# Guarding 48 small sums of squares on ScalarE instead of VectorE, in a four-block transformer kernel

## The chip, the cores and the metric

The kernel runs on one core of a Trainium2 chip. The core has five engines that each take their instructions in order: TensorE (PE, matrix products), VectorE (DVE), ScalarE (ACT), GpSimd (POOL) and SyncE (SP, which here only issues transfers). They work side by side and wait for each other through semaphores. Matrix products are written to PSUM, everything else lies in SBUF. The metric is the device time of one execution in microseconds (us); the figure before is the median of three runs.

## The reference

The input x is [4, 512, 128] in fp32. Four blocks follow each other, each as `x = x + layernorm(block(layernorm(x)))`: a linear attention, a stack of six layers of local attention and feed-forward, a dense causal attention with a softsign-like score, and a gated feed-forward. The change lies in the stack. Its attention layer, cut to what matters:

```python
def l2norm(t):
    return t / jnp.maximum(jnp.linalg.norm(t, axis=-1, keepdims=True), 1e-12)

for i in range(6):                          # 16 heads of 64, window 32
    q, k, v = split_heads(x @ Wqkv[i])
    q = rotary(l2norm(q) * q_scale[i], scale)
    k = rotary(l2norm(k) * k_scale[i], 1 / scale)
    sim = (q @ k_two_windows.T) * 8.0       # masked
    x = softmax(sim) @ v_two_windows @ Wo[i] + x
    x = ffn(layernorm(x)) + x               # gelu gate
```

For every token and head the kernel needs 1 / max(norm, 1e-12) of 64 numbers of q and of k. It takes the sum of squares, keeps it from being under 1e-24 (the guard), and forms the inverse root as exp(-0.5 ln(sum)).

## The kernel before, in words

The stack is written out as a list of steps k: six layers, four batches, two halves of eight heads (`steps`, L294), 48 in all. Each k is spread over four inner steps, so that s runs over 192 score steps, with a lead-in of ten and a tail. The loop at L681 runs over s under a manual schedule: the order of the code is the order on each engine. In each s it advances several k at once, by the offsets in `inside(s, n)`:

- `score` and `exponentials` (offset 0): for one pair of heads, a mask product (L443) and 32 small products q k (L453) into the tile sc, which has one buffer in PSUM; then VectorE's maxima (L460) and `top` (L463), and eight ACTIVATEs pr on ScalarE in two groups of four (L70), each followed by a read of the accumulator. The next s's mask product can start only when the second group of four is done.
- `project`, `rotate`, `squares`, `squared`, `rotated` (offset 10): two projections pp a step (L307), for each a multiplication by the rotary tables on VectorE (L318, tile t), the squares on ScalarE (L329, tile sq), the sums of squares over 64 columns on VectorE (L343, into ss) and the addition of the rotated halves on GpSimd (L339, tile r).
- `guarded`, `norms`, `refined`, `normed` (offset 6): the block that is changed. For each k, at its first s (`first`, when s mod 4 is 2), VectorE guards ss, 128 x 64 numbers for q and k and four token tiles, and multiplies by -0.5 (L351); ScalarE takes Ln with scale -2 and Exp with scale -0.5 (both through the helper at L70), into rn; GpSimd refines rn by one Newton step (L365 to L368, with ss again), and multiplies the keys by it (L374).
- `turn_k` (offset 4): four transposes tp on TensorE (L387), and a copy kT on ScalarE. `value` (offset 2): a product pv (L420) and a copy vn (L424).
- Offsets -1 to -4: `by_key` and `in_place` lay out the softmax weights, `weighted` forms av (L513), the copy attn (L736) takes it out of PSUM, `output` adds the product with Wo (L521).
- `parts`: the feed-forward of one layer and batch, spread over eight s by the list LATE (L526): transposes pt and px, the normalisation xt, the affine xg (L564), products pg with gelu (L578), pa (L589) and py (L599), residual additions on VectorE (L532, L606).

The period of the loop is therefore eight s: two k, one feed-forward. At s mod 8 = 7 the two copies attn and vn go to VectorE (L687); else they are on ScalarE. The PSUM tiles pp, tp, pv, pt, px, pg, pa share one pool of three banks (`mm`, L288) that go round in the order of use.

What stands in the order of the code around the change: within one s with a norm block, VectorE does the first sum of squares (L719), then the guard, then the second rotary multiplication (L733). ScalarE does the second four exponentials (L726), Ln and Exp (L728), the copies attn and vn, and the second squares (L740).

Of the kernel before, what the change touches and what calls it, by code (L numbers as in the profile page):

```python
# [8 lines left out]
F32 = mybir.dt.float32  # L9
I32 = mybir.dt.int32  # L10
BF16 = mybir.dt.bfloat16
AF = mybir.ActivationFunctionType
ALU = mybir.AluOpType
# [3 lines left out]
P = 128  # L17
# [14 lines left out]
def sandwich(ctx: ExitStack, tc: tile.TileContext, a: dict, out: bass.AP):  # L32

    nc = tc.nc
# [29 lines left out]
    def table_act(out, in_, func, **kw):  # L64
        if SETS[func] != phase["set"]:
            load_set = nc.scalar.preload_act_table_set(SETS[func])
            for name in () if phase["kept"] else phase["used"]:
                tc.add_manual_dep(load_set.ins, name, NOSYNC, reason="table phase")
            phase.update(set=SETS[func], load=load_set.ins.name, used=[])
        done = nc.scalar.activation(out, in_, func, **kw)  # L70
        if not phase["kept"]:
            tc.add_manual_dep(done.ins, phase["load"], NOSYNC, reason="table phase")
        phase["used"].append(done.ins.name)
# [24 lines left out]
    cp = stack.enter_context(tc.tile_pool(name="f0c", bufs=1))  # L98
# [31 lines left out]
    with tc.tile_pool(name="a0w", bufs=1) as awp, tc.tile_pool(name="a0", bufs=4) as work, \  # L130
# [22 lines left out]
        nc.gpsimd.tensor_copy(identb, ident)  # L153
        mhalf = cp.tile([P, 4], F32, name="mhalf")
        nc.gpsimd.memset(mhalf, -0.5)
        upper = cp.tile([P, 1], F32, name="upper")
        nc.gpsimd.memset(upper, 1.5)
        minus = cp.tile([P, 1], F32, name="minus")
# [128 lines left out]
    with tc.tile_pool(name="f0", bufs=2) as work, \  # L287
# [38 lines left out]
        def squares(k, j):  # L326
            o = proj[k]
            sq = o["sq"][j] = work.tile([P, S], F32, tag="ln_sd", name="sq")
            nc.scalar.activation(sq, o["pp"], AF.Square)  # L329
# [18 lines left out]
        def guarded(k):  # L348

            ss = proj[k]["ss"]  # L350
            nc.vector.tensor_scalar(ss, ss, 1e-24, -0.5, ALU.max, ALU.mult)  # L351

        def norms(k):

            o = proj[k]
            rn = o["rn"] = work.tile([P, 2, 4, 8], F32, bufs=3, name="rn")
            table_act(rn, o["ss"], AF.Ln, scale=-2.0)
            table_act(rn, rn, AF.Exp, scale=-0.5)
# [44 lines left out]
        def place_q(k, n):  # L403


            o = proj[k]
            if n == 0:
                o["qT"] = work.tile([P, 4, 4, 4, 32], F32, name="qT")
            for f in range(4):
                nc.sync.dma_start(  # L410
                    out=o["qT"][32 * f : 32 * f + 32, n], in_=o["qb"][32 * n : 32 * n + 32, f]
                )
# [21 lines left out]
        def score(k, p):  # L434


            o = proj[k]
            sc = scp.tile([P, 2, S], F32, tag="sc", name="sc")
            scores = o["sc"] = sc[:, :, 0 : 4 * KW].rearrange("p e (j k) -> p e j k", k=KW)
            for w in range(4):  # L440
                for e in range(2):
                    rows = slice(64 * e, 64 * e + 64)
                    nc.tensor.matmul(  # L443
                        sc[32 * w : 32 * w + 32, e, 0 : 4 * KW],
                        lhsT=identb[rows, 64 * e : 64 * e + 32], rhs=mask[rows, int(w == 0)],
                        start=True, stop=False, skip_group_check=True,
                    )
            for j in range(4):
                for w in range(4):
                    q0 = j * P + w * WIN  # L450
                    for e in range(2):
                        rows = slice(64 * e, 64 * e + 64)
                        nc.tensor.matmul(  # L453
                            scores[32 * w : 32 * w + 32, e, j, :],
                            lhsT=o["qT"][rows, w, p, j, :],
                            rhs=o["kT"][rows, p, q0 : q0 + KW],
                            start=False, stop=True, skip_group_check=True,
                        )
            raw = sc[:, 0, 4 * KW : 4 * KW + 8].rearrange("p (e j) -> p e j", e=2)
            nc.vector.tensor_reduce(raw, scores, AX.X, ALU.max, negate=True)  # L460
            top = o["top"] = work.tile([P, 2, 4], F32, name="top")
            o["rq"] = o["rn"][:, 0, :, 2 * p : 2 * p + 2]
            nc.vector.tensor_tensor(top, raw, o["rq"].rearrange("p j e -> p e j"), ALU.mult)  # L463
            o["pr"] = work.tile([P, 2, 4, KW], F32, name="pr")
            o["den"] = work.tile([P, 2, 4], F32, name="den")
# [171 lines left out]
        def inside(s, ahead):  # L637

            k, q = divmod(s + ahead, 4)
            return (k, q) if 0 <= k < len(steps) else None  # L640

        def parts(s, some):
            for part in some:
                g, left = divmod(s - LATE[part - 1], 8)
                if left or not 1 <= g <= DEPTH * NB:
                    continue
                if part < 10 or part > 13:
                    ff_part(*divmod(g - 1, NB), part)
                elif g > NB * (DEPTH - 1):
                    residual((g - 1) % NB, part - 9)  # L650
# [29 lines left out]
        with tc.manual_schedule():  # L680
            for s in range(-10, LAST + max(LATE) + 1):  # L681
                here, rot, before, flip = (inside(s, n) for n in (0, 10, 9, 9))
                fold, place, turn, val = (inside(s, n) for n in (6, 5, 4, 2))
                first = fold and fold[1] == 0

                copy = nc.scalar.copy
                if s % 8 == LATE[5] % 8 and LATE[5] < s:  # L687
                    copy = nc.vector.tensor_copy
                if place:
                    place_q(*place)  # L690
                if here:
                    score(*here)
                parts(s, (2, 5, 7, 8))
                if rot:
                    project(rot[0], 2 * rot[1])
                if here:
                    exponentials(here[0], 0)
                if rot:
                    rotate(rot[0], 2 * rot[1])
                    squares(rot[0], 2 * rot[1])  # L700
                if before:
                    squared(before[0], 2 * before[1] + 1)
                if turn:
                    turn_k(*turn)
                parts(s, (9,))
                back = inside(s, -4)
                if back:
                    i, b, hf = steps[back[0]]
                    c = 4 * hf + back[1]
                    if c == 0:  # L710
                        ff["py"] = pyp.tile([P, S], F32, name="py")
                    output(i, c, attn, ff["py"])
                if s - 1 in fresh:
                    by_keys[s - 1] = by_key(fresh.pop(s - 1))
                parts(s, (1, 3, 15))
                if s - 2 in by_keys:
                    in_place(*by_keys[s - 2])
                if rot:
                    squared(rot[0], 2 * rot[1])  # L719
                    rotated(rot[0], 2 * rot[1])  # L720
                if first:
                    guarded(fold[0])
                if rot:
                    project(rot[0], 2 * rot[1] + 1)
                if here:
                    exponentials(here[0], 1)  # L726
                if first:
                    norms(fold[0])  # L728
                back = inside(s, -3)
                if back:  # L730
                    av = weighted(*back, by_keys.pop(s - 3)[0])
                if rot:
                    rotate(rot[0], 2 * rot[1] + 1)  # L733
                if back:
                    attn = work.tile([P, S], F32, tag="attn", bufs=1, name="attn")
                    copy(attn.rearrange("p (j h c) -> p j h c", j=4, h=2), av)  # L736
                if val:
                    value(*val, copy)
                if rot:
                    squares(rot[0], 2 * rot[1] + 1)  # L740
                parts(s, (4,))
                if flip:
                    flip_q(*flip)
                if rot:
                    rotated(rot[0], 2 * rot[1] + 1)
                if here:
                    fresh[s] = normalise(here[0])
                if first:
                    refined(fold[0])
                if fold:  # L750
                    normed(*fold)
                parts(s, (14, 6, 10, 11, 12, 13))
                if here:
                    weights(*divmod(s, 32))
# [6 lines left out]
    with tc.tile_pool(name="f1w", bufs=1) as gp, tc.tile_pool(name="a1w", bufs=1) as wp, \  # L761
# [18 lines left out]
        scale = 1.0 / DH1**0.5 * 16.0  # L780
# [419 lines left out]
```

## Time and profile before

| | |
|---|---|
| median of three runs | 1991.85 us (1987.7, 1991.85, 2001.1) |
| the profiled execution | 1998.52 us, of which the span from the first to the last instruction is 1996.8 us |
| PE, DVE, ACT, POOL busy | 1812.8, 1624.7, 1603.7, 1549.5 us |
| granted TensorE clock, mean over the span | 0.957 of full |
| from 500 to 800 us: PE, DVE, ACT, POOL busy | 292.85, 268.15, 261.44, 265.13 of 300 us |
| guard L351 on DVE | 48 times, 22.2 us; 179 ns least, 182 median, 1291 most |
| Ln and Exp of the norm on ACT | 48 times each, 14.2 and 12.3 us |

In a line of a timeline the first number is the start in us from the start of the span, the second the duration in us; then engine, source line, operation, output tile <- input tiles, partitions x elements, count. A bracket at the end is the idle time of that engine just before, and what ended it. Consecutive instructions of an engine overlap a little in the profile, so a duration is somewhat longer than the distance to the next start. In a line of a group the busy time in us and the mean of one in ns follow the count, and after the second bar the idle time before them. A TensorE product of this size is two instructions, and its end is modelled.

### The profile page before, as it was taken

The numbers are of one execution on the slowest core, as the hardware profiler recorded it, in microseconds if no ns is written. First come the engines' busy times: TensorE is split into PE (matmuls) and PEld (weight loads), VectorE is DVE, ScalarE is ACT, GpSimd is POOL, SyncE is SP. The second block draws the span as 40 slices with busy tenths as digits, with TensorE's granted clock in tenths as the row PEclk, the third lists the DMA queues.
The fourth block names the chain that finished last, engine by engine and source line by source line (L and its number), as shares of the span: only waits on it lengthen the run. The fifth ranks groups of instructions, "written<-read, shape, count | busy, mean of one in ns | idle before, by whom it ended". The sixth has DMA issues, their size and how long they took to land.

```text
span 1996.8 us, 75926 instructions
## 1 busy us (share of the span) xinstructions
PE 1812.8 (91%) x30648; PEld 951.5 (48%) x30648; DVE 1624.7 (81%) x2561; ACT 1603.7 (80%) x4645; POOL 1549.5 (78%) x2026
## 2 busy tenths in 40 slices
PE   6779899999999999999999999999998877878878
PEld 3235455555555555555555555555555423323323
DVE  3698788888988898998888998889984369888833
ACT  3458788888888888888888888888888639988953
POOL 1279888888988889888898888988886338878850
PEclk9889999999999999999999999999999968889889
DMA  3023443344433444334434335333333110000000
GB/s 99 0 66 95 114 118 80 94 109 117 105 95 84 108 116 110 97 79 116 126 92 100 97 100 133 95 84 97 92 91 96 34 46 1 1 1 1 1 0 21
DMA packets 98892, 155.27 MB, mean 78 GB/s; under 512 B 29552, under 2 KB 56944, under 8 KB 93936
## 3 DMA queue, kind: packets, MB, share of 16 engines
q1 hardware_dynamic: 98544, 150.43, 29.6%
q8 instruction: 243, 3.98, 0.9%
q14 instruction: 105, 0.86, 0.2%
HBM read 23.44 MB, written 1.05 MB: 12 GB/s over the span
## 4 chain that ended last, share of the span: by engine, by line
PE 54%; ACT 19%; DVE 16%; issue 4%; SPq 4%; DMA 3%; POOL 1%; DVEq 0%; POOLq 0%; ACTq 0%
PE pp L307 10%; ACT pr L70 8%; PE av L513 6%; PE pv L420 5%; PE sc L453 5%; PE py L521 5%; PE pa L589 4%; PE pg L578 3%; PE py L599 3%; DVE la L899 3%; DVE t L318 3%; DVE lb L897 2%; ACT sq L329 2%; PE tp L387 2%; PE sc L443 2%
## 5 line engine op out<-in xcount | busy, mean ns | idle before, releaser
L70 ACT ACTIVATE pr<-sc,top,rn 128x64 f32<-128x64 f32 x1536 | 607.8, 420 | 84.5 <-DVE top L463 32.0
L339 POOL TENSOR_TENSOR r<-t 128x512 f32<-128x512 f32 x384 | 486.5, 1276 | 150.4 <-DVE t L318 132.5
L318 DVE TENSOR_TENSOR t<-pp,tab 128x1024 f32<-128x1024 f32 x384 | 467.9, 1219 | 42.8 <-PE pp L307 33.2
L307 PE MATMUL pp<-wqkv,z 128*128 128x512 f32 x768 | 412.2, 620 | 13.3 <-ACT sq L329 8.8
L70 ACT ACTIVATION_READ_ACCUMULATOR pr<-sc,top,rn 128x1 f32 x1536 | 336.3, 219 | 0.0
L329 ACT ACTIVATE sq<-pp 128x512 f32<-128x512 f32 x384 | 234.0, 609 | 89.6 <-DVE t L318 87.1
L343 DVE TENSOR_REDUCE ss<-sq 128x8 f32<-128x512 f32 x384 | 257.1, 669 | 6.6 <-ACT sq L329 4.3
L513 PEld LDWEIGHTS av<-pT,ve 64*64 64x64 f32 x6144 | 165.4, 134 | 154.6 <-POOL pT L502 46.0
L907 POOL TENSOR_TENSOR lb<-lb,la 128x2048 f32<-128x2048 f32 x40 | 182.7, 4567 | 53.8 <-issue 34.2
L420 PE MATMUL pv<-wqkv,z 128*128 128x512 f32 x384 | 217.0, 647 | 3.4 <-ACT sq L329 3.4
L479 POOL TENSOR_TENSOR pr<-pr,den 128x512 f32<-128x512 f32 x192 | 201.0, 1047 | 24.3 <-DVE den L478 22.9
L460 DVE TENSOR_REDUCE sc<-sc 128x8 f32<-128x512 f32 x192 | 131.5, 685 | 93.6 <-PE sc L453 93.0
L513 PE MATMUL av<-pT,ve 64*64 64x32 f32 x6144 | 197.6, 222 | 8.8 <-DMA qT<-qb 5.3
L307 PEld LDWEIGHTS pp<-wqkv,z 128*128 128x128 f32 x768 | 135.0, 193 | 146.5 <-issue 108.1
L374 POOL TENSOR_TENSOR r<-r,rn 128x512 f32<-128x512 f32 x192 | 200.8, 1046 | 3.8
L521 PE MATMUL py<-attn,wo 128*128 128x512 f32 x384 | 197.0, 594 | 1.5 <-ACT attn L736 1.5
L513 PE MATMUL av<-pT,vn 64*64 64x32 f32 x6144 | 193.7, 219 | 0.0
L453 PE MATMUL sc<-kT,qT 64*32 64x64 f32 x12288 | 171.1, 223 | 8.7 <-issue 8.7
L503 POOL COPY pT<-blocks 32x256 f32<-32x256 f32 x384 | 152.4, 397 | 22.3
L513 PEld LDWEIGHTS av<-pT,vn 64*64 64x64 f32 x6144 | 166.3, 135 | 0.1
L453 PEld LDWEIGHTS sc<-kT,qT 64*32 64x32 f32 x12288 | 154.5, 105 | 10.0 <-issue 9.5
L502 POOL COPY pT<-blocks 32x256 f32<-32x256 f32 x384 | 150.3, 391 | 11.1 <-issue 2.9
(195 smaller groups left out, 3271.2 us busy)
## 6 DMA issues: line engine op xcount, KB each, us to landing
qT<-qb SPq DMA_DIRECT2D x768, 64.0 KB
ve<-vn SPq DMA_DIRECT2D x48, 768.0 KB
pT<-blocks SPq DMA_DIRECT2D x768, 32.0 KB
wqkv<-in_f_wqkv SPq DMA_DIRECT2D x36, 256.0 KB
ve<-vn SPq DMA_DIRECT2D x48, 192.0 KB
tab<-in_rot SPq DMA_DIRECT2D x12, 256.0 KB
wo<-in_f_wo SPq DMA_DIRECT2D x6, 512.0 KB
ve<-vn SPq DMA_DIRECT2D x48, 64.0 KB
```

Of the source, the lines that this page charges most:

```text
L70: done = nc.scalar.activation(out, in_, func, **kw)
L307: nc.tensor.matmul(pp, lhsT=z[b][:, WIN + t * P : WIN + (t + 1) * P], rhs=ws[i]["qkv", hf][:, n * S : (n + 1) * S], start=True, stop=True,)
L318: nc.vector.tensor_tensor(t12, o["pp"].rearrange("p (h d) -> p h d", d=DH0).unsqueeze(1) .to_broadcast([P, 2, 8, DH0]), ws[i][f"tab{n}"][: ...
L329: nc.scalar.activation(sq, o["pp"], AF.Square)
L339: nc.gpsimd.tensor_tensor(r, t1, t2[:, :, ::-1, :], ALU.add)
L343: nc.vector.tensor_reduce(o["ss"][:, n, t, :], o["sq"].pop(j).rearrange("p (h d) -> p h d", d=DH0), AX.X, ALU.add,)
L374: nc.gpsimd.tensor_tensor(v, v, o["rn"][:, 1, t].unsqueeze(2).to_broadcast([P, 8, DH0]), ALU.mult)
L420: nc.tensor.matmul(pv, lhsT=z[b][:, WIN + t * P : WIN + (t + 1) * P], rhs=ws[i]["qkv", hf][:, 2 * S :], start=True, stop=True,)
L453: nc.tensor.matmul(scores[32 * w : 32 * w + 32, e, j, :], lhsT=o["qT"][rows, w, p, j, :], rhs=o["kT"][rows, p, q0 : q0 + KW], start=False, ...
L479: nc.gpsimd.tensor_tensor(o["pr"], o["pr"], o["den"].unsqueeze(3).to_broadcast([P, 2, 4, KW]), ALU.mult)
L513: nc.tensor.matmul(av[64 * e : 64 * e + 64, h, 64 * j + 32 * c : 64 * j + 32 * c + 32], lhsT=vs[c][rows, j, (2 * p + e) * DH0 : (2 * p + e ...
L521: nc.tensor.matmul(py, lhsT=ws[i]["wo"][:, c, :], rhs=t, start=(c == 0), stop=(c == 7))
```

## The change

The guard no longer runs on VectorE. In its place ScalarE does two operations in front of Ln. The first is Relu(ss - 1e-24), the second is Identity(-0.5 y - 0.5e-24), which gives -0.5 max(ss, 1e-24) together. Both take their constant from a column of a new tile `under`, which GpSimd fills at the start. The call of `guarded` moves from between the first sum of squares and the second projection to just in front of `norms`, behind the second group of exponentials. Ln then waits for ScalarE's own Identity in place of VectorE's guard, and Relu waits for VectorE's last sum of squares of that k, which is early in the same s.

```diff
         mhalf = cp.tile([P, 4], F32, name="mhalf")
         nc.gpsimd.memset(mhalf, -0.5)
+        under = cp.tile([P, 2], F32, name="under")
+        nc.gpsimd.memset(under[:, 0:1], -1e-24)
+        nc.gpsimd.memset(under[:, 1:2], -0.5e-24)
...
         def guarded(k):
             ss = proj[k]["ss"]
-            nc.vector.tensor_scalar(ss, ss, 1e-24, -0.5, ALU.max, ALU.mult)
+            nc.scalar.activation(ss, ss, AF.Relu, bias=under[:, 0:1])
+            nc.scalar.activation(ss, ss, AF.Identity, bias=under[:, 1:2], scale=-0.5)
...
                     rotated(rot[0], 2 * rot[1])
-                if first:
-                    guarded(fold[0])
                 if rot:
                     project(rot[0], 2 * rot[1] + 1)
                 if here:
                     exponentials(here[0], 1)
                 if first:
+                    guarded(fold[0])
                     norms(fold[0])
```

## The prediction

> **What bounds the kernel now.** I read the page first (shares, slices, chain), then the chain of waits in order of time, then the timelines of TensorE, ScalarE, VectorE and GpSimd around single instances of the changed step, and last the groups of the instructions involved.
>
> ```profile
> PE 1812.8 (91%) x30648; PEld 951.5 (48%) x30648; DVE 1624.7 (81%) x2561; ACT 1603.7 (80%) x4645; POOL 1549.5 (78%) x2026
> PE   6779899999999999999999999999998877878878
> PEclk9889999999999999999999999999999968889889
> PE 54%; ACT 19%; DVE 16%; issue 4%; SPq 4%; DMA 3%; POOL 1%; DVEq 0%; POOLq 0%; ACTq 0%
> ```
>
> The stack is the stretch from about 105 to 1510 us. TensorE (PE) is full there and has its full clock, so the time is lost or won where TensorE stalls. The chain names ScalarE (ACT) second. From 500 to 800 us TensorE is busy 292.9 of 300 us, VectorE (DVE) 268.2, ScalarE 261.4, GpSimd (POOL) 265.1: four engines at nearly 90%, so small shifts decide.
>
> The steps repeat in periods of eight (one layer and batch), near 60 us. The norm block runs twice in each: at s mod 8 = 6 ("place six") and s mod 8 = 2 ("place two"). ScalarE and TensorE at place six, s=78:
>
> ```profile
> 722.45 0.25 ACT L70 ACTIVATION_READ_ACCUMULATOR pr<-sc,top,rn 128x1 f32 x1
> 722.61 0.26 ACT L70 ACTIVATE rn<-ss 128x64 f32<-128x64 f32 x1
> 722.89 0.26 ACT L70 ACTIVATE rn<-rn 128x64 f32<-128x64 f32 x1
> 723.06 0.57 ACT L736 COPY attn<-av 128x512 f32<-128x512 f32 x1
> 723.52 0.59 ACT L424 COPY vn<-pv 128x512 f32<-128x512 f32 x1
> 724.00 0.61 ACT L329 ACTIVATE sq<-pp 128x512 f32<-128x512 f32 x1
> 724.49 0.79 ACT L564 ACTIVATE xg<-px,par 128x512 f32<-128x512 f32 x1
> ...
> 723.63 0.66 PE L562 MATMUL px<-ident,xt 128*128 128x128 f32 x4
> 724.17 1.13 PE L307 MATMUL pp<-wqkv,z 128*128 128x512 f32 x2
> ```
>
> The reader is to see that ScalarE has no gap here, and that the vn copy ends at 724.11 and the next pp product starts at 724.17. In the built program that product waits for this very copy: the three mm banks go round, and it takes the bank that the copy empties. So TensorE is already level with ScalarE at place six. I looked at the 21 such places from s=14 to s=174: in 16 the product starts 0.05 to 0.13 us after the copy, in 2 (s=62, 102) 0.35 and 0.44 us after, in 3 (s=46, 126, 166) 1.0 to 1.2 us after.
>
> **Removed: the guard on VectorE.**
>
> ```profile
> L351 DVE TENSOR_SCALAR ss<-ss 128x64 f32<-128x64 f32 x48 | 22.2, 462 | 0.0
> L70 ACT ACTIVATE rn<-ss 128x64 f32<-128x64 f32 x48 | 14.2, 295 | 1.7 <-DVE ss L351 1.7
> 721.29 1.28 DVE L351 TENSOR_SCALAR ss<-ss 128x64 f32<-128x64 f32 x1
> 722.49 1.21 DVE L318 TENSOR_TENSOR t<-pp,tab 128x1024 f32<-128x1024 f32 x1
> 721.26 1.26 POOL L339 TENSOR_TENSOR r<-t 128x512 f32<-128x512 f32 x1
> 781.62 0.18 DVE L351 TENSOR_SCALAR ss<-ss 128x64 f32<-128x64 f32 x1
> ```
>
> The guard takes 0.18 us in 31 of 48 cases, but over 1 us in 13: at 721.29 it starts 0.03 us after a GpSimd addition and ends with it. The Trainium skill ("SBUF — State Buffer", Who interferes with whom) says that a tensor_scalar can take the port pair that VectorE shares with GpSimd, as an exclusive lock, and that the later one blocks for the other's whole instruction. The rows agree (1.28 against 1.26 us). By that rule the change frees 22.2 - 48 x 0.18 = 13.6 us of stalls, and with 0.09 us of issue for each guard (752.24 to the next start at 752.33) about 18 us of VectorE. If VectorE set the end that would be 18 us won. The trace has the test in it. Of the 21 places six, 13 have a long guard and 8 a short one. From the mask product (L443) of step 7 to that of step 8 it is 9.36 us at best and 9.37 at the median with a long guard (9.38 at s=78, 722.75 to 732.13), and 9.36 at best and 9.37 at the median with a short one. One microsecond of VectorE is worth nothing there, since its next critical product, top, waits for the scores from TensorE, and ScalarE is still busy with xg when top is ready. At place two the guard is always short, and VectorE waits for TensorE before its maxima (0.18 us at 754.43). ScalarE waited for the guard 1.7 us in all, in the two runs ahead of the first scores. I take the removal at 0; bounds 18 us won and 0. What it does move is GpSimd's second addition of r at place six (1.26 us idle at 723.78, waiting for L318), up to 1.2 us earlier; the next one waits for a new pp anyway.
>
> **Added: Relu and Identity on ScalarE.** 48 of each, 128x64, each with a bias column and waiting for the one before it. The trace has no Relu; the nearest rows are the two ACTIVATEs of the same shape and the same kind of chain: Ln to Exp, start to start, is 0.28 to 0.34 us but for one of 0.40, median 0.33. In front of the chain two more links cost 2 x 0.33 = 0.66 us. The low bound is 2 x 0.28 = 0.56. For the high bound I take the Identity that has two columns (L555, four in 1.64 us at 716.99): 2 x 0.41 = 0.82. A rule of the Trainium skill speaks against the change: "ScalarE: Activation LUTs", Rules for kernel authors, sends relu, max, add and mul to VectorE. The same page (What ACT_TABLE_LOAD costs) gives an ACTIVATE with a bias column as 280 + 0.833 N ns, 333 at N = 64, with 93 of it overlapped back to back: an estimate of 0.48 us for the two. The trace's dependent pair doesn't overlap like that, so I keep 0.66. Busy time grows by 48 x 2 x 0.3 = 29 us, to about 82% of the span; what matters is where it lies.
>
> The pair stands behind the exponentials whose end releases the next scores, so that release doesn't move. Queued behind it are Ln, Exp, the attn and vn copies, sq, and xg at place six. Who waits for these:
>
> Place six: the pp product of step 7 waits for vn with nothing to spare. 16 x 0.66 = 10.6 us, less 0.1 for the two looser ones; s=62 pays 0.66 - 0.30 = 0.36 and s=102 pays 0.27; three pay nothing. Together 11.1 us. It isn't paid twice: ScalarE runs the same 0.66 us late through the gelu group of step 7 up to the exponentials of step 8. I find no later slack that takes it back, since TensorE goes from px at 723.63 to step 9 with hardly a gap, and what stalls it later (step 5) hangs on pp products that move along.
>
> Place two: ScalarE has a gap of 0.17 us before the exponentials of step 3, which takes 0.17; 0.49 goes on to the scores of step 4. The tp transposes of step 3 wait for vn and have about 0.45 to spare. But the exponentials of step 4 wait for VectorE, which runs without a stop from 755.56 (s=83) through the residual additions, and ScalarE has 0.73 + 0.40 us of gaps there:
>
> ```profile
> 761.33 0.60 ACT L329 ACTIVATE sq<-pp 128x512 f32<-128x512 f32 x1 [0.73 <-DVE t L318]
> 762.80 0.40 ACT L70 ACTIVATE pr<-sc,top,rn 128x64 f32<-128x64 f32 x1 [0.40 <-POOL r L339]
> 767.04 0.30 PE L443 MATMUL sc<-mask,identb 64*32 64x256 bf16 x8 [0.50 <-ACT pr L70]
> ```
>
> TensorE, 0.49 late, then meets the stall of 0.50 us that it has at 767.04 anyway (0.36 to 0.50 in most periods). So place two costs 0 to 0.13 us; I take 0.05 x 23 = 1.2 us. Without that cover it would be about 19 x 0.49 = 9.3 us, since some four periods have a wider gap.
>
> The rest: two memsets of one column on GpSimd before the stack, beside an idle engine, 0 (bounds 0 and 0.5). GpSimd's refinement (L365) now follows an Exp 0.66 us later; it starts 1.8 us or more after Exp ends in the instances that I read, so 0. No table load is added: the built program holds as many as before, and the trace runs L555's Identity between exponentials without one. No DMA or queue moves.
>
> Sum: 11.1 + 1.2 + 0 = 12.3 us. The profiled execution took 1998.5 us (span 1996.8 and 1.7 around it); the runs' median is 1991.85, 6.7 lower, and I put the sum on that: **2004 us**. With 0.56 us for the pair it is 9.3, with 0.82 it is about 17.5; with 3 us of scatter the case spans 1998 to 2012.
>
> **The rivals.**
>
> Place two is paid too. The cover there is thin: 0.49 us against a stall of 0.36 to 0.50. If VectorE's chain in step 4 moves along with the scores, both places cost: 12.3 + 9.3 = 21.6 us, 2013.5, up to 2018 with a dearer pair. For it: the spare time is only just enough, and tp is nearly level as well. Against: the maxima of step 4 start at 761.86 although the scores were done at 760.73.
>
> VectorE's relief decides (faster). With the 18 us freed and the pair hidden by ScalarE's gaps: 1974. It begins to count if top of step 7 is what holds the exponentials, that is if ScalarE reaches them before VectorE. Against it: the equal steps under long and short guards, and zero gap on ScalarE at place six.
>
> The delay is absorbed. TensorE loses 0.66 us at step 7 and gets it back in a stall further on whose source doesn't move, a transfer say: 1992, give or take 4. For it: some steps stretch irregularly (9.6 to 10.4 us for step 7 in 7 of 21 places), so there are other waits. Against: in the regular periods none is in the chain.
>
> That it doesn't do what it says: if either function needed its own table, two loads of 1.28 us in each block would add over 120 us; the unchanged number of loads excludes it.
>
> **How the numbers follow.** Place six alone 0.58 (2004), both places 0.20 (2014), absorbed 0.15 (1992), faster 0.07 (1974). One per cent, 20 us, is about what a measurement of this kernel tells from no change. Below 1972 lies half of the faster case: 0.03. Above 2012 lie most of the second case and the top of the first: 0.19. The rest, 0.78, is within. For 8 in 10 the range runs from 1988 to 2016, which leaves out the faster case, the edge of the absorbed one and the dear end of the second.
>
> **What would show it.** Right: new rows L354 and L355 on ScalarE, x48, near 0.3 us each, and no guard on VectorE; the pp product of step 7 idle for about 0.6 us because of the vn copy; step 7 near 10.0 instead of 9.36 us; step 3 longer by 0.5 and step 4 shorter by as much. Wrong: step 7 unchanged (absorbed or never exposed), step 4 as long as before with step 3 longer (both places paid), or any step shorter than before by about 1 us (VectorE counted after all).

## The result and the profile after

The changed kernel takes 2006.8 us (median of nine runs, 1997.5 to 2014.2). The kernel before takes 1988.8 in nine runs of its own. The ratio is 1.0076, with a 95% interval of 1.0055 to 1.0098: slower by 15 us (11 to 19; the medians lie 18 us apart). That is clear of the noise, since the interval leaves out 1, and still within the one per cent that the prediction called "same". The forecast was 12.3 us more, 2004, in a range of 1988 to 2016.

The page of the profile after (span 2012.5 us against 1996.8; the profiled execution is the slowest of the nine), with the busy times and the chain of waits by engine:

```profile
PE 1820.5 (90%) x30648; PEld 951.9 (47%) x30648; DVE 1608.3 (80%) x2513; ACT 1632.5 (81%) x4741; POOL 1547.3 (77%) x2028
PE 51%; ACT 20%; DVE 15%; issue 5%; SPq 4%; DMA 3%; POOL 1%; DVEq 0%; POOLq 0%; ACTq 0%
```

TensorE's share of the chain has gone from 54 to 51%, and ScalarE's from 19 to 20%. The groups of the norm block on ScalarE (count, then busy time in us, mean of one in ns, idle time before them):

```profile
L354 ACT ACTIVATE ss<-ss,under 128x64 f32<-128x64 f32 x48 | 18.7, 390 | 0.0
L355 ACT ACTIVATE ss<-ss,under 128x64 f32<-128x64 f32 x48 | 16.7, 349 | 1.6
L70 ACT ACTIVATE rn<-ss 128x64 f32<-128x64 f32 x48 | 12.3, 257 | 1.5
```

VectorE's busy time has fallen by 16 us (the guards were 22.2) and ScalarE's has grown by 29. The pair takes 0.39 and 0.35 us, more than the 0.3 that the prediction gave each.

Place six (s=78) after the change, in the timelines of ScalarE, TensorE and VectorE:

```profile
725.42 0.39 ACT L354 ACTIVATE ss<-ss,under 128x64 f32<-128x64 f32 x1
725.84 0.35 ACT L355 ACTIVATE ss<-ss,under 128x64 f32<-128x64 f32 x1
726.22 0.26 ACT L70 ACTIVATE rn<-ss 128x64 f32<-128x64 f32 x1
726.51 0.26 ACT L70 ACTIVATE rn<-rn 128x64 f32<-128x64 f32 x1
726.67 0.57 ACT L739 COPY attn<-av 128x512 f32<-128x512 f32 x1
727.14 0.59 ACT L428 COPY vn<-pv 128x512 f32<-128x512 f32 x1
...
725.63 0.30 PE L447 MATMUL sc<-mask,identb 64*32 64x256 bf16 x8 [0.50 <-ACT pr L70]
726.51 0.66 PE L566 MATMUL px<-ident,xt 128*128 128x128 f32 x4
727.78 1.12 PE L310 MATMUL pp<-wqkv,z 128*128 128x512 f32 x2 [0.61 <-ACT vn L428]
735.75 0.30 PE L447 MATMUL sc<-mask,identb 64*32 64x256 bf16 x8
...
726.62 0.70 DVE L464 TENSOR_REDUCE sc<-sc 128x8 f32<-128x512 f32 x1 [0.52 <-PE sc L457]
```

The vn copy ends at 727.73 and the pp product starts at 727.78, 0.05 us later; before it was 0.06. But TensorE has now been idle for 0.61 us, which the profile puts down to this copy. From mask product to mask product step 7 takes 10.12 us; it took 9.38. The views of waits hold the same for the whole run (us in total, times, longest). The first line has no counterpart in the kernel before, and of the second there was one instance, of 0.4 us:

```profile
PE pp L310 <- ACT vn L428: 10.9, 19, 0.6
PE tp L391 <- ACT vn L428: 4.1, 18, 0.3
```

The second line is place two: the transposes of step 3 wait for vn as well, but for less. The mask products of TensorE around place two (s=82 to 85), with these transposes and ScalarE's last read of the accumulator in step 3:

```profile
750.81 0.30 PE L447 MATMUL sc<-mask,identb 64*32 64x256 bf16 x8
757.06 0.30 PE L447 MATMUL sc<-mask,identb 64*32 64x256 bf16 x8
759.31 0.63 PE L391 MATMUL tp<-ident,r 128*128 128x128 f32 x4 [0.23 <-ACT vn L428]
763.45 0.27 ACT L70 ACTIVATION_READ_ACCUMULATOR pr<-sc,top,rn 128x1 f32 x1
763.77 0.30 PE L447 MATMUL sc<-mask,identb 64*32 64x256 bf16 x8
770.65 0.30 PE L447 MATMUL sc<-mask,identb 64*32 64x256 bf16 x8
```

Step 3 takes 6.71 us where 6.24 stood before, and step 4 takes 6.88 in place of 7.36: what step 3 loses, step 4 gives back. Two ways lead to the 6.71, and they arrive almost together. The mask product of step 4 starts 0.05 us after the last read has ended (763.72), as it did before (759.63, then 759.68); in 18 of the 21 periods after the change, and 18 before, that distance is 0.04 to 0.06 us, and ScalarE's exponentials of step 3 end 0.47 us later here. On TensorE the product pv in front of it starts at 762.65, 1.12 us ahead, where 1.05 to 1.06 is the distance without a wait (steps 1 and 5). So the exponentials hold it for only 0.07 us, and the wait of the transposes alone would have made step 3 nearly as long. The profile shows no idle time here, since the modelled end of pv reaches up to the mask product.

The median of each step of the period, in us from mask product to mask product, over the periods from s=14 to s=181, for both kernels:

| | 0 | 1 | 2 | 3 | 4 | 5 | 6 | 7 | sum |
|---|---|---|---|---|---|---|---|---|---|
| before | 7.12 | 7.94 | 6.25 | 6.32 | 7.35 | 8.80 | 6.83 | 9.37 | 59.98 |
| after | 7.12 | 7.94 | 6.24 | 6.72 | 6.88 | 8.80 | 6.82 | 10.12 | 60.64 |

A period is 0.66 us longer; 21 of them make 13.9 us. Added up over all steps of the two profiled executions it is 15.7 us: step 7 gives 12.0, step 3 gives 12.9, step 4 takes back 9.7, and the rest is 0.5. The 3.2 us of steps 3 and 4 together come from a few stretched steps (s=147: 6.24 before, 10.48 after; s=27 and 107: 7.73 and 8.26 before, 10.12 and 10.45 after). In these three steps after the change TensorE stands for 2.3 to 2.6 us with nothing that the profile shows it to wait for ("issue"); before, it did so at s=27 and 107 for 1.4 and 1.8 us. What holds it there stays open.

### The profile page after: what moved, and what is told of

Same layout as the page of the kernel before. It is cut to its first block, busy times and chain, and to the rows that moved or that the text cites. A ratio compares the mean times of both kernels' runs of the same rounds, so it can differ in the third digit from the quotient of the medians.

```text
span 2012.5 us, 76022 instructions
## 1 busy us (share of the span) xinstructions
PE 1820.5 (90%) x30648; PEld 951.9 (47%) x30648; DVE 1608.3 (80%) x2513; ACT 1632.5 (81%) x4741; POOL 1547.3 (77%) x2028
## 3 DMA queue, kind: packets, MB, share of 16 engines
HBM read 23.44 MB, written 1.05 MB: 12 GB/s over the span
## 4 chain that ended last, share of the span: by engine, by line
PE 51%; ACT 20%; DVE 15%; issue 5%; SPq 4%; DMA 3%; POOL 1%; DVEq 0%; POOLq 0%; ACTq 0%
PE pp L310 10%; ACT pr L70 8%; PE av L517 6%; PE pv L424 5%; PE py L525 4%; PE sc L457 4%; PE pa L593 3%; PE pg L582 3%; PE py L603 3%; DVE la L902 2%; DVE lb L900 2%; PE tp L391 2%; ACT sq L332 2%; DVE t L321 2%; ACT lb L70 2%
## 5 line engine op out<-in xcount | busy, mean ns | idle before, releaser
L70 ACT ACTIVATION_READ_ACCUMULATOR pr<-sc,top,rn 128x1 f32 x1536 | 342.8, 223 | 0.0
```

## The experiments

The theory: ScalarE is later by the length of the pair; at place six this reaches TensorE in full, at place two a gap and a stall take it, and VectorE's relief is worth nothing. Against it stand: place two is paid too; the relief matters and is buried under a larger loss; and a question inside the theory, whether the bank that vn empties is the only way to TensorE or ScalarE's whole row is late.

**The pair at place six alone.** The second place keeps the guard of before, at its old place on VectorE (`on_vector`).

```diff
+                if first and fold[0] % 2 != 1:
+                    on_vector(fold[0])
...
                 if first:
-                    guarded(fold[0])
+                    if fold[0] % 2 == 1:
+                        guarded(fold[0])
                     norms(fold[0])
```

> The pair is on ScalarE only for odd k, that is at place six; at place two the guard stays on VectorE where it was. If the cost is place six's alone: step 7 is 10.12 us as with the full change (9.36 before), steps 3 and 4 are as before (6.3 and 7.35), and the time is 11 to 13 us over the kernel before, about 2001. If place two is paid too, this kernel gets only half of the full change's 15 to 18 us: about 1997.

Measured: 2004.7 us against 1990.3, ratio 1.0076 (1.0049 to 1.0103). Step 7 is 10.12, steps 3 and 4 are 6.33 and 7.28, the period is 60.65. The whole cost of the change is in this half of it.

**The pair at place two alone** (the same edit with even and odd exchanged).

> The pair is on ScalarE only for even k, that is at place two; at place six the guard stays on VectorE. If place two is covered: step 3 is 0.46 us longer, step 4 is 0.47 shorter, step 7 stays at 9.36, and the time is within 3 us of the kernel before. If place two is half of the cost: 7 to 9 us slower than before.

Measured: 1990.1 us, ratio 1.0004 (0.9986 to 1.0021). Step 3 is 6.72, step 4 is 6.88, step 7 is 9.36, the period is 59.88. Place two is covered.

**Four operations at place two.** As the last one, with two more in the chain:

```diff
             nc.scalar.activation(ss, ss, AF.Identity, bias=under[:, 1:2], scale=-0.5)
+            for _ in range(2):
+                nc.scalar.activation(ss, ss, AF.Identity, bias=under[:, 1:2])
```

> As the run with the pair at place two alone, but with two more Identity there (they add 1e-24 and are otherwise without effect), four in the chain instead of two, about 1.55 us of delay. If the cover at place two is 0.17 us of ScalarE's gap and about 0.5 us of TensorE's stall: step 3 is about 1.3 longer, step 4 can give back only about 0.5, and the time is 14 to 19 us over the kernel before. If the cover is wide (VectorE's chain): no cost again, within 4 us.

Measured: 2009.9 us against 1990.0, ratio 1.0092 (1.0059 to 1.0125), 18 us. Step 3 is 7.48 (1.16 longer), step 4 is 6.71 (0.64 shorter), step 5 is 9.33 (0.53 longer); the period is 61.00, 1.02 us over before. In the timeline of TensorE the transposes now wait 1.00 us for vn:

```profile
756.73 0.30 PE L454 MATMUL sc<-mask,identb 64*32 64x256 bf16 x8
759.74 0.63 PE L398 MATMUL tp<-ident,r 128*128 128x128 f32 x4 [1.00 <-ACT vn L435]
764.21 0.30 PE L454 MATMUL sc<-mask,identb 64*32 64x256 bf16 x8
771.11 0.30 PE L454 MATMUL sc<-mask,identb 64*32 64x256 bf16 x8
```

As after the change, ScalarE's last read of step 3 ends 0.05 us before the mask product of step 4 (764.16), so that both ways are late together. Step 5 is 9.2 to 9.4 us in 14 of the 21 periods and under 8.9 in the others, the one shown among them; why was not followed. The cover is thin: of about 1.5 us of delay, some 0.5 us is taken and the rest is paid. The change stayed inside it by little.

**No guard.** The guard is dropped; the factor and the sign go where they cost nothing.

```diff
-            nc.scalar.activation(sq, o["pp"], AF.Square)
+            nc.scalar.activation(sq, o["pp"], AF.Square, scale=0.5**0.5)
...
-            table_act(rn, o["ss"], AF.Ln, scale=-2.0)
+            table_act(rn, o["ss"], AF.Ln, scale=2.0)
...
-            nc.gpsimd.tensor_tensor(tn, tn, upper.to_broadcast([P, 2 * 4 * 8]), ALU.add)
+            nc.gpsimd.tensor_tensor(tn, upper.to_broadcast([P, 2 * 4 * 8]), tn, ALU.subtract)
...
-                if first:
-                    guarded(fold[0])
```

> No guard at all: left out is the floor of 1e-24 under the sums. The factor 0.5 goes into the scale of the squares and the sign into a subtraction in the refinement, so that VectorE's guard is gone and ScalarE gets nothing for it. If VectorE's relief is worth nothing: within 3 us of the kernel before. If the freed 18 us of VectorE count: 1971 to 1980, and the full change would then hold a loss of some 30 us on ScalarE.

Measured: 1989.1 us against 1990.3, ratio 0.9983 (0.9962 to 1.0004). The steps are 7.12, 7.94, 6.25, 6.35, 7.35, 8.80, 6.84 and 9.37, a period of 60.02. TensorE's mask products of steps 7 and 8 at s=79:

```profile
712.50 0.30 PE L443 MATMUL sc<-mask,identb 64*32 64x256 bf16 x8 [0.37 <-ACT pr L70]
721.87 0.30 PE L443 MATMUL sc<-mask,identb 64*32 64x256 bf16 x8
```

With the guard gone from VectorE and nothing added to ScalarE, step 7 is the same 9.37 us. The relief is worth nothing in a regular period; the interval leaves at most 7.5 us for the irregular ones. So the change's cost isn't the rest of a gain and a larger loss.

**The norm block behind the second squares.** All four operations are moved; nothing else changes.

```diff
                 if first:
-                    guarded(fold[0])
-                    norms(fold[0])
...
                     squares(rot[0], 2 * rot[1] + 1)
+                if first:
+                    guarded(fold[0])
+                    norms(fold[0])
```

> All four operations of the norm block (the pair, Ln, Exp) stand behind the copies attn and vn and behind the second squares, so the bank of vn is free 1.3 us earlier than in the changed kernel. If the bank is the only way in which the delay reaches TensorE: the product pp of step 7 is on time again, step 7 is back at about 9.4 and the time at about 1990. If ScalarE's whole row through step 7 is late as the prediction says, so that the gelu products wait for its squares instead: step 7 stays at 10.0 to 10.2 and the time at 2003 to 2008.

Measured: 2000.7 us, ratio 1.0044 (1.0024 to 1.0065). Step 7 is 9.78: neither 9.4 nor 10.0 to 10.2, half way. TensorE in step 7 (s=79):

```profile
714.67 0.30 PE L447 MATMUL sc<-mask,identb 64*32 64x256 bf16 x8 [0.36 <-ACT pr L70]
716.05 1.02 PE L310 MATMUL pp<-wqkv,z 128*128 128x512 f32 x2
721.19 1.02 PE L582 MATMUL pg<-xg,w 128*128 128x512 f32 x2
722.54 1.98 PE L582 MATMUL pg<-xg,w 128*128 128x512 f32 x4 [0.33 <-ACT sq L332]
724.46 0.30 PE L447 MATMUL sc<-mask,identb 64*32 64x256 bf16 x8
```

The pp product is on time (1.38 us after the mask product; 2.15 in the changed kernel, 1.42 before). Now the second gelu product waits 0.33 us for the squares of step 7, which come late because ScalarE's row is late. There are two ways to TensorE: the bank of vn, which has no slack, and ScalarE's row through step 7, which has about 0.35 us. In the changed kernel the first stall hides the second.

**Without bias columns.** The floor becomes zero, which is what is left out.

```diff
-            nc.scalar.activation(ss, ss, AF.Relu, bias=under[:, 0:1])
-            nc.scalar.activation(ss, ss, AF.Identity, bias=under[:, 1:2], scale=-0.5)
+            nc.scalar.activation(ss, ss, AF.Relu)
+            nc.scalar.activation(ss, ss, AF.Identity, scale=-0.5)
```

> The changed kernel with Relu and Identity without bias columns: left out is the 1e-24, so that the floor is zero. If the columns are what made the pair 0.76 instead of 0.66 us: the two take about 0.26 us each, step 7 is 9.9 to 10.0 (0.56 to 0.6 over before) and the time is about 3 us under the changed kernel. If Relu and Identity are slow by themselves: 0.35 and 0.39 again and no difference.

Measured: 2000.2 us, ratio 1.0050 (1.0036 to 1.0063), and step 7 is 9.94. The groups:

```profile
L354 ACT ACTIVATE ss<-ss 128x64 f32<-128x64 f32 x48 | 14.3, 299 | 0.0
L355 ACT ACTIVATE ss<-ss 128x64 f32<-128x64 f32 x48 | 12.3, 257 | 1.5
```

Against 390 and 349 ns with a column: 0.09 us for each column. Relu and Identity themselves are as fast as Ln and Exp.

**One operation of the pair** (the line with Relu is taken out, and with it the floor).

> The changed kernel without Relu: left out is the floor, and one operation with a bias column is left of the pair. If the cost is ScalarE's delay at place six one to one: step 7 is 9.73 to 9.78 (0.38 to 0.42 over before), and the time is about half way, 6 to 8 us over the kernel before. If there is a threshold, it is all or nothing: 9.36 or 10.12.

Measured: 1996.4 us, ratio 1.0033 (1.0017 to 1.0049). Step 7 is 9.74. No threshold.

**The floor in Ln.** As without a guard, but `table_act(rn, o["ss"], AF.Ln, bias=under, scale=2.0)` with a column of 1e-24.

> As the kernel without a guard operation, but the floor comes in as a bias column of 1e-24 in Ln, so that nothing is left out but the exact form of the maximum. If a bias column costs ScalarE some 0.1 us in an operation: step 7 is 0.05 to 0.1 longer than without it, 1 to 2 us in all, and the time is within 4 us of the kernel before. If Ln hides it: no difference to the kernel without a guard.

Measured: 1994.6 us, ratio 1.0015 (0.9995 to 1.0034), Ln at 390 ns in place of 298 without the column, and step 7 at 9.45. Together with the others this gives the dose at place six: the further ScalarE time in front of vn, and what step 7 gains over the 9.37 us without a guard.

| in front of vn | later by (us) | step 7 longer by (us) |
|---|---|---|
| a column in Ln | 0.09 | 0.08 |
| one operation with a column | about 0.38 | 0.37 |
| the pair without columns | about 0.58 | 0.57 |
| the pair with columns | about 0.76 | 0.75 |

The middle column is worked out from starts: at s=78 the pair takes 0.42 + 0.38 = 0.80 from Relu's start to Ln's, and Ln to Exp is 0.29 where 0.33 was the median before, so 0.76. The pair without columns is that less 2 x 0.09; one operation is 0.42 less 0.04. The traces bear it out: from the mask product of step 7 to the end of vn the medians are 1.34 us without a guard, and 1.43, 1.72, 1.92 and 2.10 down the rows.

**The floor in Ln, and the block behind the squares.** The last two ideas together (Ln and Exp moved as above).

> As the kernel with the floor in Ln's bias column, with Ln and Exp behind the copies and the second squares. If TensorE is the limit at place six once ScalarE gives the bank early: step 7 goes from 9.45 back to 9.36 and no lower, and the time is that of the kernel before or up to 4 us less. If ScalarE's row is still the limit there: step 7 stays at 9.45. If the block held TensorE up even before the change: step 7 falls under 9.3 and the time by more than 4 us.

Measured: 1991.5 us against 1989.7, ratio 1.0003 (0.9987 to 1.0019). No expectation fits whole: step 7 is 9.25, as for a block that held TensorE up even before the change, but the time has not fallen. The two instructions of the pp product start at 718.07 and are followed by tp at 718.93, 0.86 us; before, they were at 724.17 and 725.13, 0.96. Of the 0.12 us that step 7 is shorter than in the kernel before, 0.1 is this pair: the bank cost TensorE that much already there. Over 21 periods that is about 2 us, and the total doesn't show it. None of these kernels is measurably faster than the one before.

## Why the prediction was right

**What bounds.** Right. TensorE sets the steps, and what counts is who makes it wait. Step 7 is longer by 0.75 us although TensorE does the same work.

**The removal at 0.** Right, and shown: without any guard all eight steps keep their length. The long guards of over a microsecond, blocked behind GpSimd, were real; VectorE then simply waits for TensorE. After the change it waits 0.52 us for the scores at 726.62, a wait that wasn't there at s=78. The comparison of places with long and short guards, made inside one trace, had the answer before the run. The bound of 18 us for the relief falls.

**The pair at 0.66.** Too small, by the bias columns. This term explains why step 7 is 0.75 us longer instead of 0.64 to 0.66. I took the distance from Ln to Exp, which have no column, for two operations that have one. The columns add 2 x 0.09. The Trainium skill ("ScalarE: Activation LUTs", What ACT_TABLE_LOAD costs) has a figure for just this, about 93 ns for each pointer operand, and the runs show 0.09. The prediction quoted the page's total with a column and dropped it, since its overlap of back-to-back operations doesn't hold for a dependent chain. The row without a column and the page's step for one should have been put together, to an estimate of 2 x (0.33 + 0.09) = 0.84 us; 0.80 was seen from Relu to Ln.

**Place six pays in full.** Right in mechanism and size: 16 x 0.66 + 0.6 was 11.1 us; the steps 7 add up to 12.0. The two places with 0.35 and 0.44 us of slack paid 0.56 and 0.47 (forecast 0.36 and 0.27): 0.1 of the difference is the bias columns, and 0.1 the pp product itself, which took 0.86 us there with its bank free early and takes 0.96 now. Of the 16 without slack, two paid less, since their step was stretched before already (0.42 and 0.01), and one more (1.29). The three with a microsecond of slack came out at 0.57, -0.14 and -0.30, on average nothing as forecast, with a scatter of the executions on top. The wait is the one named, pp for vn.

**Not paid twice, and ScalarE equally late through step 7.** The first holds. The second was put too strongly: ScalarE's row has about 0.35 us of slack in step 7, seen when the block stands behind the squares. The bank is the sharper of the two.

**Place two covered.** Right. The way forecast, through the exponentials of step 3, is the one that ends last, but only by 0.07 us; the transposes' wait for vn, which the prediction took to have 0.45 us to spare, would have done nearly the same. Step 3 is longer by 0.40 at the median, 0.47 at s=82 (forecast 0.49), step 4 shorter by 0.47, and alone it has a ratio of 1.0004 (0.9986 to 1.0021). With twice the operations this place is paid.

**The sum.** 12.3 us forecast, 15 measured (11 to 19). Of the 15.7 between the two profiled executions 12.0 are step 7 (forecast 11.1). The 3.2 of steps 3 and 4 (forecast 1.2) come from the stretched steps, which its sum does not hold; that the 1.2 has the same sign is chance.

## What to carry to other kernels

A small operation costs what stands behind it in its engine's queue: look for the copy or release with no slack that follows, and compare the end of that copy with the start of its consumer. In this kernel two operations of 0.4 us on an engine that is 80% busy cost nearly their full length once in a period and nothing in the other place, while the 22.2 us of guards taken off VectorE were worth nothing in a regular period. Before such a change, look in the trace for places where the same operation happens to be long and short, and compare what follows: that is the experiment, already run.

## What I had not expected

A bias column costs an ACTIVATE of 128x64 0.09 us: 349 against 257 ns inside a chain, 390 against 299 at its head. The first operation of a chain takes 0.04 us more than the next, whichever it is: Ln is 0.298 us at the head (without a guard) and 0.257 behind Identity. Behind the squares the head takes 0.42 with its column, not 0.39. And a product that waits for its bank up to the last moment loses 0.1 us more than the wait: the pair of pp instructions took 0.96 us with the bank just in time, and 0.86 with it free early. The kernel before has both in one trace: 0.86 at four places six where the copy had ended 0.35 us or more ahead (s=46, 62, 102 and 126), and 0.92 to 0.97 where it had ended within 0.1. Why is open.
